# Two matrix sums change places in PSUM: the down projection of layer 0 moves from the convolution's banks to those of the transposed maxima

## Chip, cores and metric

The kernel runs on one core of one Trainium2 chip. The metric is the device time of one execution in microseconds (us). The engines are called PE (TensorE, with its weight loads as PEld), DVE (VectorE), ACT (ScalarE), POOL (GpSimd) and SP (SyncE, which issues transfers). PSUM is the memory into which PE writes and from which DVE and ACT read.

## What is computed

Two layers are applied to x, 32 graphs of 512 nodes with 256 features, with a 0/1 adjacency of 512 x 512 for each graph. The change lies in layer 0, which is a graph convolution and then a feed-forward block, each behind a layer norm and added to x. Cut to what matters:

```python
# graph convolution
h = x @ W_msg
msg_sum = einsum('bij,biu->bju', a, h);  deg = sum(a, axis=1)
out = relu(x @ W_upd + msg_sum / max(deg, 1) + bias)          # 0 for deg == 0
# feed-forward block, for each node
t = max(xx[:, None, :] + Wt[None, :, :], axis=-1) + bt         # 1024 maxima over 256 sums
trop = s * max_k(t * sl_cvx + of_cvx) + (1 - s) * min_k(t * sl_ccv + of_ccv)
classical = gelu(x @ Wc + bc);  g = sigmoid(x @ Wg + bg)
fused = g * trop + (1 - g) * classical
out = fused @ Wd + bd                                          # the down projection
```

Layer 1 (attention over typed edges, then a mixer with a scan over slices) isn't touched.

## The kernel before

Layer 0 is `layer0_sorted`. Nodes are in tiles of P = 128 rows; a group has NT = 4 tiles, 512 nodes; the 1024 features of the block are FC = 8 chunks of 128. The 32 graphs are in 4 segments of 8. A segment's nodes are first convolved, then ordered by how many of their features can hold the maximum (`put_in_order`), and then taken in 8 groups, so there are 32 groups in all. CAPS says how many rows of a table are gathered for each of a segment's tiles: 24, 9, 7, ... down to 1.

The convolution of a graph is two generators. `conv_in` loads the graph and its adjacency, norms it, and multiplies by W_msg: tiles `ph` (L403), copied to `h` by ACT (L405). `conv_out` runs over pairs of node tiles: `pu` (L421) is the product with W_upd, which DVE adds to the bias into `u` (L424); for each of the two tiles `pm` (L430) is the sum over neighbours, which DVE turns into `deg` (L433, L434) and adds to `u` (L435).

The feed-forward block of a group is three functions:

- `sums(s, g)` gathers the ordered nodes `xs` (POOL, L549), norms and transposes them (`xsp`, L573), gathers rows of the table (`best` L560, `rows` L591) and takes their maximum on DVE (`best`, L594).
- `mixed(s, g)` runs over the 8 chunks f. For each it multiplies by Wc and Wg (`clsp` and `gatep`, L619) and lets ACT apply gelu and tanh (`cls`, `gate`, L621); PE transposes the maxima of the four node tiles into `tz` (L626); ACT reads tz once for the first line of the piecewise function (`acc`, L628) and once for each bend (`past`, L632; BENDS has 6, 3, 2, 1, 1, 1, 0, 0 of them); DVE adds the bends (L633) and mixes the parts (L635 to L637) into `acc[f]`, which has one buffer for each f.
- `down(s, g)` multiplies acc by Wd, two node tiles at a time, into a tile `po` (L648: 2 tiles x 8 chunks), which DVE adds to xs (L650); SP then writes the group to `x2s` (L651).

In the text tz6 is the tile tz of chunk f = 6, acc7 the tile acc of chunk 7, and so on.

The order in which the code writes the work of a group: the loop over groups takes the first step of `mixed` of the group (clsp and gatep of f = 0), then `down` of the group before it, and then weaves the other steps of `mixed` with `sums` of the next group. The generator `woven` does that by counting steps, and a second `woven` lays the convolution of the next segment beside the whole; once all convolutions are done, the same stream goes on with the preparation of layer 1 (`following`). That is the written order. The order in which each engine gets its instructions is fixed when the program is built, and differs from it in places.

PSUM has one pool for all of layer 0, `ps`, with two buffers for each tag, and each tile of the pool has 2 KiB per partition, one bank. The tags are

- `tp`: transposes of normed nodes (lnp, xsp) and of weights,
- `mm`: the convolution's ph, pu, pm, the three tiles of `put_in_order`, a few tiles of layer 1's preparation, and po,
- `mf`: clsp and gatep,
- `tz`: the transposed maxima tz.

A tile takes a bank when the earlier tile of its tag in that bank has been read for the last time; for po this is the add at L650, for tz the last read by ACT (L628 or L632).

Of the kernel before, what the change touches and what calls it, by code (L numbers as in the profile page):

```python
# [8 lines left out]
F32 = mybir.dt.float32  # L9
# [9 lines left out]
P = 128  # L19
N = 512  # L20
D = 256
# [75 lines left out]
def layer0_sorted(tc, ident, eps, x, adj, w, x2s, ranks, over, following):  # L97
# [29 lines left out]
    with ExitStack() as ctx:  # L127
        cst = ctx.enter_context(tc.tile_pool(name="c0", bufs=1))
        dr = ctx.enter_context(tc.tile_pool(name="d0", bufs=2, space=DRAM))
        ps = ctx.enter_context(tc.tile_pool(name="p0", bufs=2, space=PSUM))  # L130
# [408 lines left out]
        def feed_forwards():  # L539
# [101 lines left out]
            def down(s, g):  # L641
                xg, acc = got.pop((s, g))
                for t0 in range(0, NT, 2):
                    po = ps.tile([P, 2, D], F32, tag="mm", name=f"po{s}_{g}_{t0}")
                    for i in range(2):
                        t = t0 + i
                        for f in range(FC):
                            nc.tensor.matmul(po[:, i, :], acc[f][:, t * P : (t + 1) * P], wd[:, f, :],  # L648
                                             start=f == 0, stop=f == FC - 1)
                    nc.vector.tensor_add(xg[:, t0 : t0 + 2, :D], xg[:, t0 : t0 + 2, :D], po)  # L650
                nc.sync.dma_start(x2s[s].rearrange("(t k p) d -> k p t d", k=NG, p=P)[g], xg[:, :, :D])  # L651
# [6 lines left out]
            for i, now in enumerate(groups):  # L658
                steps_ = mixed(*now)
                next(steps_)  # L660
                if i:
                    down(*groups[i - 1])
                yield
                more = sums(*groups[i + 1]) if i + 1 < len(groups) else iter(())
                steps = sum(1 + CAPS[n] // 4 for n in range(groups[(i + 1) % len(groups)][1], ST, NG))
                yield from woven(steps_, 9, more, steps)
            down(*groups[-1])

        def all_convs():
# [1565 lines left out]
```

## Time and profile before

| | us |
|---|---|
| median of 3 runs | 4599.11 |
| lowest and highest | 4596.14, 4614.08 |
| the profiled execution | 4612.24 |
| its span, first to last instruction | 4610.5 |

Busy times in the span: PE 4079.0 us (88%), PEld 2518.9 (55%), DVE 3368.3 (73%), ACT 2292.1 (50%), POOL 1733.9 (38%). The mean granted clock of PE is 0.950.

The stages of the span: up to 404 us the first convolutions and the tables; from 404.2 us, where the first po starts, to about 1902 us groups woven with convolutions; up to about 2114 us groups beside layer 1's preparation; up to 2498 us the last groups; after that layer 1. One group takes some 60 to 78 us while convolutions run beside it, and 53 us near the end.

The instructions of the down projection are 2048 records of matmuls of 128x128 by 128x256 on PE (a matmul in this number format leaves two records) with a median of 379 ns, overlapping, so that the 64 records of a group take 14.0 us, and 64 adds on DVE with a median of 681 ns.

How to read the lines below. A line of waits says which instruction waited for which, the total in us, how many times, and the longest. A line of the timeline has start and duration in us, the engine, the source line, the operation, the tiles written and read, how many instructions were merged into the line, and in brackets how long the engine had been idle before it and what ended that. Ends of matmuls are modelled, and a busy PE isn't PE at its peak. Half of the 64 matmul records of a group belong to the first po, half to the second.

### The profile page before, as it was taken

Reading aid. Unit: us, or ns where it says so; the run is one execution under the profiler, and the core shown is the slowest. Engines: PE = TensorE matmul, PEld = TensorE weight load, DVE = VectorE, ACT = ScalarE, POOL = GpSimd, SP = SyncE. Lnnn points to the kernel's source line nnn. Section 1 sums busy time; section 2 is a strip of 40 time slices with the busy share of each in tenths; the row PEclk is TensorE's granted clock in tenths of the full one; section 3 lists DMA queues with packets and bytes.
Section 4 is the critical chain, followed back from the end, with each engine's and each line's share of the span. In section 5 each row is a group of like instructions: output and inputs, shape, how many; then the busy total and the mean of one; then the engine's idle time right before and its main releaser. Section 6 shows DMA issues by size and latency. Waiting matters only on the chain. (4 is left out here: it accounts for less than half of the span.)

```text
span 4610.5 us, 56109 instructions
## 1 busy us (share of the span) xinstructions
PE 4079.0 (88%) x19287; PEld 2518.9 (55%) x19287; DVE 3368.3 (73%) x6944; ACT 2292.1 (50%) x4756; POOL 1733.9 (38%) x2036
## 2 busy tenths in 40 slices
PE   5668898989989899888897899999999999999987
PEld 4545665656656566555554355555555555555555
DVE  6668778877788777777775777777777776777773
ACT  2344565555655556555564444545554454454433
POOL 2356544654537444353332223223323333332220
PEclk9888999999999999998998999999999999999998
DMA  5556533654427543374431111111111111111100
GB/s 130 160 162 208 170 125 115 204 181 138 137 95 223 171 131 127 91 261 147 137 110 49 53 46 56 51 48 42 45 56 49 56 56 53 48 54 56 40 14 15
DMA packets 235099, 474.08 MB, mean 103 GB/s; under 512 B 38299, under 2 KB 114075, under 8 KB 234804
## 3 DMA queue, kind: packets, MB, share of 16 engines
q0 software_dynamic: 80256, 282.38, 19.2%
q1 hardware_dynamic: 154548, 188.02, 13.3%
q8 instruction: 154, 2.52, 0.2%
q14 instruction: 141, 1.16, 0.1%
HBM read 413.16 MB, written 57.16 MB: 102 GB/s over the span
## 5 line engine op out<-in xcount | busy, mean ns | idle before, releaser
L619 PE MATMUL clsp<-xnT,wc 128*128 128x512 f32 x1024 | 526.6, 633 | 76.5 <-ACT cls L621 56.4
L619 PE MATMUL gatep<-xnT,wg 128*128 128x512 f32 x1024 | 500.7, 608 | 3.7 <-ACT gate L621 3.4
L648 PE MATMUL po<-wd,acc 128*128 128x256 f32 x2048 | 454.2, 381 | 3.9 <-DVE acc L637 2.2
L648 PEld LDWEIGHTS po<-wd,acc 128*128 128x128 f32 x2048 | 389.8, 191 | 69.4 <-issue 12.9
L430 PE MATMUL pm<-h,adj 128*128 128x257 f32 x1024 | 294.6, 434 | 126.4 <-DVE u L435 46.7
L633 DVE SCALAR_TENSOR_TENSOR acc<-past,fld,acc 128x512 f32<-128x512 f32 x448 | 347.9, 779 | 62.7 <-ACT past L632 52.6
L1209 DVE SCALAR_TENSOR_TENSOR att<-own,other,mask 128x512 f32<-128x512 f32 x512 | 376.5, 757 | 14.1 <-DMA own<-ownd 13.8
L594 DVE SCALAR_TENSOR_TENSOR best<-rows,xs,best 128x1024 f32<-128x1024 f32 x212 | 274.2, 1296 | 148.4 <-ACT best L588 93.2
L628 ACT ACTIVATE acc<-tz,fld 128x512 f32<-128x512 f32 x256 | 198.5, 776 | 283.1 <-PE tz L626 283.1
L619 PEld LDWEIGHTS gatep<-xnT,wg 128*128 128x128 f32 x1024 | 198.8, 197 | 249.7 <-issue 209.0
L591 POOL DMA_INDIRECT rows<-table,xs x212 | 253.0, 1193 | 215.7 <-DVE best L594 160.3
L632 ACT ACTIVATE past<-tz,fld 128x512 f32<-128x512 f32 x448 | 290.7, 691 | 76.6 <-DVE acc L633 76.0
L430 PEld LDWEIGHTS pm<-h,adj 128*128 128x128 f32 x1024 | 211.7, 217 | 186.2 <-issue 106.0
L1242 PE MATMUL avp<-att,hv 128*64 128x512 f32 x1024 | 308.7, 625 | 4.2 <-DVE att L1209 4.2
L619 PEld LDWEIGHTS clsp<-xnT,wc 128*128 128x128 f32 x1024 | 188.3, 201 | 226.4 <-issue 121.3
L1330 PE MATMUL lgp<-wsl,x4T 128*128 128x512 f32 x512 | 256.0, 637 | 29.8 <-DVE mask L1081 24.3
L621 ACT ACTIVATE cls<-clsp,fld 128x512 f32<-128x512 f32 x256 | 175.1, 684 | 208.6 <-PE clsp L619 102.3
L1342 PE MATMUL yTp<-sw,x 128*128 128x512 f32 x512 | 243.7, 617 | 36.4 <-DVE sw L1337 29.0
L1150 POOL DMA_INDIRECT x<-x2s,ranks x128 | 141.6, 1106 | 345.9 <-DVE att L1209 112.3
L621 ACT ACTIVATE gate<-gatep,fld 128x512 f32<-128x512 f32 x256 | 175.4, 685 | 140.2 <-PE gatep L619 105.4
L1295 POOL TENSOR_TENSOR mu<-mu,eps 128x16 f32<-128x16 f32 x32 | 121.1, 3784 | 324.4 <-DVE mu L1294 323.2
L549 POOL DMA_INDIRECT xs<-rows_of,order x128 | 145.7, 1138 | 229.6 <-DVE acc L633 82.0
(598 smaller groups left out, 8944.0 us busy)
## 6 DMA issues: line engine op xcount, KB each, us to landing
adji<-in_adj SPq DMA_DIRECT2D x128, 256.0 KB
ai<-in_adj SPq DMA_DIRECT2D x128, 256.0 KB
own<-ownd SPq DMA_DIRECT2D x128, 256.0 KB
rows_of<-keep SPq DMA_DIRECT2D x32, 550.0 KB
x<-in_x SPq DMA_DIRECT2D x32, 512.0 KB
x2s<-xs SPq DMA_DIRECT2D x32, 512.0 KB
out<-x SPq DMA_DIRECT2D x32, 512.0 KB
rows<-table,xs POOLq DMA_INDIRECT x212
```

Source lines behind the costliest of these rows:

```text
L430: nc.tensor.matmul(pm[:, : D + 1], a[:, i, t * P : (t + 1) * P], h[:, i, :], start=i == 0, stop=i == NT - 1)
L591: nc.gpsimd.indirect_dma_start(out=row, out_offset=None, in_=table, in_offset=bass.IndirectOffsetOnAxis(ap=idxs[:, k : k + 1].bitcast(U32) ...
L594: nc.vector.scalar_tensor_tensor(m, row, vals[:, k : k + 1], m, ALU.add, ALU.max)
L619: nc.tensor.matmul(pf, wf[:, c, f * P : (f + 1) * P], xnT[:, c, :], start=c == 0, stop=c == DC - 1)
L621: nc.scalar.activation(o, pf, fn, bias=fld[:, f, bf : bf + 1], scale=1.0 if fn == AF.Gelu else 0.5)
L632: nc.scalar.activation(r, z, AF.Relu, bias=fld[:, f, AT + b : AT + b + 1])
L633: nc.vector.scalar_tensor_tensor(y, r, fld[:, f, CH + b : CH + b + 1], y, ALU.mult, ALU.add)
L648: nc.tensor.matmul(po[:, i, :], acc[f][:, t * P : (t + 1) * P], wd[:, f, :], start=f == 0, stop=f == FC - 1)
L1209: nc.vector.scalar_tensor_tensor(e, own[h], other[:, j, h : h + 1], mask[:, j, :], ALU.max, ALU.mult)
L1242: nc.tensor.matmul(pv[q][k * HO : (k + 1) * HO, :], hv[:, j, h, :HO], weighed[b, h, j], start=j == 0, stop=j == NT - 1)
L1330: nc.tensor.matmul(pf, xnT[:, c, t * P : (t + 1) * P], wsl[:, c, :], start=c == 0, stop=c == DC - 1)
L1342: nc.tensor.matmul(py, xn[:, t, c * P : (c + 1) * P], sw[:, t, :], start=t == 0, stop=t == NT - 1)
```

## The change

The tile po is taken from the tag tz instead of mm. Shape, type, matmuls, the add and everything around stay as they are:

```diff
             def down(s, g):
                 xg, acc = got.pop((s, g))
                 for t0 in range(0, NT, 2):
-                    po = ps.tile([P, 2, D], F32, tag="mm", name=f"po{s}_{g}_{t0}")
+                    po = ps.tile([P, 2, D], F32, tag="tz", name=f"po{s}_{g}_{t0}")
                     for i in range(2):
                         t = t0 + i
                         for f in range(FC):
```

Both tags have two buffers of one bank each, so the pool stays at eight banks.

## The prediction

> **What bounds the kernel now.** Layer 0 ends at about 2498 us of the span of 4610.5 us (the last add of the down projection starts at 2497.4 us), and the change touches nothing later. So I read layer 0 alone: first the busy times by stretch, then PE's waits in one stretch, then the timeline around one down projection. The chain of waits is of no use here, because it follows the end of the kernel, deep in layer 1.
>
> From the windows (length, then busy time of PE, PEld, DVE, ACT, POOL), the stretch in which convolutions and feed-forward groups are woven:
>
> ```profile
> core 0: us, PE busy (x) PEld busy (x) DVE busy (x) ACT busy (x) POOL busy (x), PEclk, DMA share, GB/s
> 404.20:1902.50 1498.30, 1355.22 (x5104) 892.80 (x5103) 1170.54 (x2327) 828.25 (x1431) 750.62 (x1006) 0.96 0.47 150
> ```
>
> PE is busy for 90% of it and idle for 143 us; DVE 78%, ACT 55%. What PE's idle time waits for, in the same stretch:
>
> ```profile
> engine line waited for: us in total, times, longest us
> PE pm L430 <- DVE xs L650: 40.4, 14, 6.0
> PE pm L430 <- DVE u L435: 35.8, 11, 6.4
> PE clsp L619 <- ACT cls L621: 23.0, 22, 2.3
> PE tz L626 <- ACT acc L628: 9.1, 11, 2.3
> PE ph L403 <- DVE xs L650: 8.7, 2, 4.4
> ```
>
> The first and fifth lines are the change's target: the convolution's matmuls pm and ph wait for the adds at L650, which empty po. The only thing that they share with po is the pair of banks of tag mm. It is 49.1 us in 16 waits, a third of PE's idle time. One of the 16 closely, first PE, then DVE, then ACT:
>
> ```profile
> 1264.37 12.68 PE L648 MATMUL po<-wd,acc 128*128 128x256 f32 x58
> 1276.88 1.89 PE L421 MATMUL pu<-w_upd,x1T 128*128 128x256 f32 x8
> 1280.45 1.98 PE L430 MATMUL pm<-h,adj 128*128 128x257 f32 x8 [1.68 <-DVE xs L650]
> 1282.27 0.60 PE L626 MATMUL tz<-ident,best 128*128 128x128 f32 x4
> ```
>
> ```profile
> 1272.80 0.68 DVE L650 TENSOR_TENSOR xs<-xs,po 128x512 f32<-128x512 f32 x1
> 1274.61 1.28 DVE L594 SCALAR_TENSOR_TENSOR best<-rows,xs,best 128x1024 f32<-128x1024 f32 x1 [1.12 <-DMA rows<-table,xs]
> 1277.20 2.51 DVE L594 SCALAR_TENSOR_TENSOR best<-rows,xs,best 128x1024 f32<-128x1024 f32 x2 [1.30 <-DMA rows<-table,xs]
> 1279.62 0.68 DVE L650 TENSOR_TENSOR xs<-xs,po 128x512 f32<-128x512 f32 x1
> 1282.47 0.16 DVE L433 TENSOR_SCALAR deg<-pm 128x1 f32<-128x1 f32 x1 [1.56 <-PE pm L430]
> ```
>
> ```profile
> 1282.91 0.78 ACT L628 ACTIVATE acc<-tz,fld 128x512 f32<-128x512 f32 x1 [10.98 <-PE tz L626]
> ```
>
> The second po is full at 1277.05 us, but its add stands in DVE's queue behind maxima (L594) that wait for gathered rows; it runs 2.6 us late. pu takes the first po's bank, pm the second's, so pm waits; then DVE waits 1.56 us for pm, and the transposes tz and ACT behind them are late too.
>
> **What the Trainium skill says.** "PSUM — Partial Sum Buffer", "Specifications (TRN2)", gives 8 banks of 2 KiB per partition. The pool has four tags of two such tiles, so all eight are taken and po can only move, not get banks of its own. The same page, "Engine vs sequencer instructions": matmuls start and complete in program order, and VectorE's queue is strictly first in, first out. The trace agrees: nothing on PE passes the waiting pm at 1280.45, and the add at 1279.62 passes no L594. "Perfetto Trace Analysis", "Optimization Strategy", says that the same gap, repeating on the engine that should be saturated, can mean too little PSUM for the next tile; the 16 waits are such a gap.
>
> **The change part by part.** No instruction is added or removed: 64 po tiles (32 groups, two each), 2048 matmul records, 64 adds of 0.68 us stay.
>
> Removed: the 16 waits. In order of time they are 3.23, 2.72, 2.63, 1.32, 4.44, 5.22, 3.48, 2.74, 2.39, 1.68, 4.30, 5.99, 2.41, 2.73, 1.15 and 2.71 us, 49.1 together. How much survives depends on what PE waits for next:
> - In four groups (3.23, 2.63, 2.39, 1.15: 9.4 us) no larger wait for DVE follows before the next group, and DVE itself waits 1.6 to 3.2 us there for pm or for past from ACT. I keep all 9.4.
> - In four groups (4.44, 5.22, 4.30, 5.99: 20.0 us), those with the many rounds of maxima, DVE is nearly as full as PE: 67.6 against 67.7 us busy in 836 to 911 us, 61.3 against 65.2 in 911 to 984. I keep half, 10.0.
> - In the other eight (19.8 us) PE waits again within about 20 us, 2.9 to 6.4 us for u at L435, and there DVE had been held by "over" at L602, which waits for the gathered xs (32.6 us in 10 waits). PE's gain mostly makes that wait longer. I keep a third, 6.6.
> Sum 26.0 us.
>
> Added: po now takes the two banks that tz6 and tz7 of its own group had. po's f=7 matmul needs acc7, which DVE makes after ACT has read tz7, and tz6 was read before, so this wait costs nothing. Behind po, tz0 of the next group takes the first po's bank and waits for the first add; tz1 waits for the second. The first add ends before the second po is full in every group (closest: it ends at 1149.21 us, and the transposes start at 1149.24), so that wait costs nothing. The second add ends up to 8.2 us after po, and tz1 is reached 3.9 us after po where only tz0, cls and gate lie between, later where convolution work does. Comparing the add's end with the start of tz1 as it stands, less the removed wait, three groups pay: 425.98 against 423.94 us (2.0), 2142.65 against 2140.36 (2.3) and 2197.74 against 2194.09 (3.7). The last, PE and DVE:
>
> ```profile
> 2194.09 0.60 PE L626 MATMUL tz<-ident,best 128*128 128x128 f32 x4
> ...
> 2200.97 3.71 PE L619 MATMUL clsp<-xnT,wc 128*128 128x512 f32 x4 [6.17 <-ACT cls L621]
> ```
>
> ```profile
> 2197.06 0.68 DVE L650 TENSOR_TENSOR xs<-xs,po 128x512 f32<-128x512 f32 x1
> ```
>
> Here, and in the second (4.24 us for cls after it), the next PE wait is longer than the new one and swallows it; if that cover were gone it is 5.9 us more. I charge 2.0.
>
> Moved: the order of work on an engine is not the written one, and it can be drawn anew. Now, transposes of the next group often run ahead of po (three of tz0, three of tz1):
>
> ```profile
> 544.96 0.49 PE L626 MATMUL tz<-ident,best 128*128 128x128 f32 x3
> 545.97 0.55 PE L626 MATMUL tz<-ident,best 128*128 128x128 f32 x3 [0.53 <-ACT acc L628]
> ```
>
> They come before the po that starts at 554.57 us. Counting the transposes before each po, 74 run ahead like this. I assume that the banks of one tag go out in the order of the code, po first; the other way both tz tiles would hold the banks, ACT could not empty them, since acc0 has one buffer that po has yet to read, and the program could not run. So the 74 fall behind po: 74 x 0.11 us (what one adds in a run of them) = 8 us of PE work, which now fills the time before po. Against it, the waits tz on acc (9.1 us, mostly this run-ahead) go, and pu, pm and ph may now be put before a po that waits. The trace can't show that order. I take zero; bounds are 9 gained and 8 lost.
>
> Net 26.0 - 2.0 = 24 us. The profiled execution takes 4612.24 us around its span of 4610.5, so it would become about 4588; it lies 13 us over the median shown, so the median goes from 4599.1 to 4575.
>
> **The rivals.**
> - Everything stays gained: PE is the bound at 90%, and 49 + 9 - 2 = 56 at most, 49 as its middle: 4550. For it: the PE share. Against it: the L435 waits and the full DVE.
> - All is absorbed: DVE and the row gathers set the pace, the stall at pm turns into waits of PE for u or cls: 4597, 10 either way. For it: 20 of the 49 us stand ahead of such waits.
> - Slower: transposes that no longer run ahead. If the new order puts tz1 right behind tz0, cls and gate, it waits for the second add wherever that starts more than 3.3 us after po's end (3.9 less 0.68): summed over the groups' present lags, 23 us. With the 8 us of transposes that is 31, and ACT and DVE, which can start acc0 only after them, pass it on; with 8 of the 49 us kept it is 23 slower, 4622. It decides once the adds lag behind po by more than these 3.3 us in most groups; today they do in 16 of 32.
>
> **How the numbers follow.** Forecast (4575, own range 4558 to 4590) 0.42; all gained 0.16; absorbed 0.22; slower 0.20. What a measurement here can tell from no change is about 0.5%, 23 us, so faster means below 4576. Of the forecast's 0.42, 0.27 lies below it; with the 0.16, faster is 0.43. Same: 0.15 of the forecast, 0.20 of absorbed, 0.03 of slower, 0.38. Slower: 0.17 and 0.02, 0.19. The range leaves out the better half of "all gained" and the worse half of "slower": 4540 to 4625.
>
> **What would show it.** Right: no wait of pm or ph on L650; waits of PE for L650 only at tz, below 10 us; the last add of L650 some 24 us before 2497; layer 1 as long as before. Waits of pm for u at L435 above 36 us show the absorbed part. Wrong: tz waiting for L650 in most groups, or PE busy before po with nothing and after it with eight transposes; or a change in layer 1's length, which would mean that the order there was redrawn.

## The result: no measurable change

The changed kernel takes 4608.6 us (median of 20 runs) beside 4609.2 us for the kernel before (20 runs). The ratio is 1.0003, with a 95% interval of 0.9994 to 1.0012. The forecast of 4575 us was 34 us too low: 10 of them because it started from a median of 3 runs, 4599.1 us, and 24 because the gain didn't come. The profiled execution has a span of 4604.4 us (4610.5 before) at nearly the same mean granted clock, 0.952 for 0.950. Layer 0 ends 9 us earlier in it (the last matmul of po ends at 2488.3 us, before at 2497.3), layer 1 takes 3 us longer.

What was meant to go is gone. First the windows over the same stretch of groups and convolutions (length, busy time of each engine), then PE's waits there, both of the changed kernel:

```profile
404.20:1902.50 1498.30, 1344.95 (x5100) 880.68 (x5099) 1175.37 (x2324) 831.05 (x1434) 757.11 (x1006) 0.96 0.47 150
```

```profile
PE pm L430 <- DVE u L435: 59.1, 16, 7.9
PE clsp L619 <- ACT cls L621: 45.6, 31, 4.8
...
PE tz L626 <- DVE xs L650: 3.1, 5, 1.6
```

The 49.1 us of pm and ph behind the adds have left, and only 3.1 us of tz behind them came. Yet PE is no busier than before (1345 us for 1355). Two other waits grew by nearly as much as was saved: pm for u at L435 from 35.8 to 59.1 us, and clsp for cls from 23.0 to 45.6 us.

The group that the prediction followed (group 12, counted from 0) shows the first of them. PE, DVE and POOL of the changed kernel, as timelines:

```profile
1276.81 1.88 PE L619 MATMUL gatep<-xnT,wg 128*128 128x512 f32 x4
1284.78 3.77 PE L430 MATMUL pm<-h,adj 128*128 128x257 f32 x8 [6.09 <-DVE u L435]
```

```profile
1266.36 0.68 DVE L650 TENSOR_TENSOR xs<-xs,po 128x512 f32<-128x512 f32 x1
...
1277.64 0.17 DVE L602 TENSOR_TENSOR over<-xs,limits 128x4 f32<-128x4 f32 x1 [5.20 <-DMA xs<-rows_of,order]
...
1284.16 0.48 DVE L435 SCALAR_TENSOR_TENSOR u<-pm,deg,u 128x256 f32<-128x256 f32 x1
```

```profile
1270.75 0.95 POOL L549 DMA_INDIRECT xs<-rows_of,order  x1 [10.48 <-DVE acc L633]
```

The same compare and the same pm in the kernel before:

```profile
1291.65 0.17 DVE L602 TENSOR_TENSOR over<-xs,limits 128x4 f32<-128x4 f32 x1 [4.03 <-DMA xs<-rows_of,order]
```

```profile
1298.78 3.77 PE L430 MATMUL pm<-h,adj 128*128 128x257 f32 x8 [4.92 <-DVE u L435]
```

Read the changed kernel's lines upwards. The matmul pm waits 6.09 us for u, which is a 0.48 us operation. It stands in DVE's queue behind the compare `over` at L602, 0.17 us long, and behind 6.4 us of other work that piled up after it, while the compare itself stood 5.20 us waiting for the rows xs of a later group. POOL could issue the gather of those rows at 1270.75 us only. The bracket names an acc of DVE, but xs has three buffers, so the rows of group 15 need the one of group 12, whose adds must be done and whose write (L651) must have left: in both kernels the gather starts 3.69 us after SP issues that write (1267.06 and 1270.75 after, 1280.34 and 1284.03 before). So the stall at the adds and this one are links of one chain that starts with the second add: from that add to the compare it takes 12.0 us before (1279.62 to 1291.65) and 11.3 us after (1266.36 to 1277.64). When the add comes earlier, the compare comes as much earlier, but PE, which has lost its first pause, arrives earlier too, and waits here: 6.09 us, where it had waited 4.92.

### The profile page after: what moved, and what is told of

It reads as the page before. It is cut to its first block, busy times and chain, and to the rows that moved or that the text cites. A ratio compares the mean times of both kernels' runs of the same rounds, so it can differ in the third digit from the quotient of the medians.

```text
span 4604.4 us, 56098 instructions
## 1 busy us (share of the span) xinstructions
PE 4069.8 (88%) x19287; PEld 2509.9 (55%) x19287; DVE 3368.6 (73%) x6944; ACT 2291.6 (50%) x4756; POOL 1741.5 (38%) x2036
## 5 line engine op out<-in xcount | busy, mean ns | idle before, releaser
L619 PE MATMUL clsp<-xnT,wc 128*128 128x512 f32 x1024 | 524.9, 633 | 85.4 <-ACT cls L621 70.2
```

Source lines behind the costliest of these rows:

```text
L619: nc.tensor.matmul(pf, wf[:, c, f * P : (f + 1) * P], xnT[:, c, :], start=c == 0, stop=c == DC - 1)
```

## The experiments

The recorded expectations name theories by letters, each with what it claims. The main ones are A (the compare at L602 takes the place of the stall), D (DVE is too full to let anything be gained), G (the stall is worth some 30 us, and sharing the bank tz costs as much; its opposite F says that L602 absorbs all of it), with two ideas of where that cost lies: G2 and G2a (transposes and classifier products no longer run ahead of po) and G3 (the order on the engines is drawn anew in layer 1's preparation). Each ratio is against the kernel before on the same chip, with its 95% interval. Where two kernels are compared by their ratios, the two intervals leave about 10 us either way (an estimate from them).

### The compare, PE and a third way to empty po

Two kernels without the compare at L602: its flags are set to zero once, so the marking of nodes that need more rows than were gathered is left out. One starts from the kernel before (b_noover), the other from the changed one (a_noover).

```diff
-                nc.vector.tensor_tensor(over[...], xg[:, :, COUNT], limits[...], ALU.is_gt)
...
             got = {}
+            nc.gpsimd.memset(over[:, : B * NT], 0.0)
```

> The kernel before without the compare at L602 (leaves out the flags of rows whose list was too short; they are set to zero instead). It takes away the place where DVE waits for the gathered xs (67.4 us in 18 waits), nothing else. Theory A (PE's gain from the change is absorbed because DVE stands at L602, in a chain of fixed length that starts at the second add of po): PE's waits of pm for u at L435 fall from 46.7 to under 25 us and the time falls by 15 to 40 us. Theory B (PE is the bound, and the change gave back its gain by its own costs: transposes that no longer run ahead, waits at tz): the time stays within 8 us. Theory C (DVE and the row gathers are the bound as a whole, L602 is one wait among many): L602's time goes to other DVE waits, less than 10 us gained.

> The changed kernel without the compare at L602 (leaves out the same flags). Theory A: with the place of absorption gone, the change is worth something: a_noover is faster than b_noover by 10 to 25 us (the 19.8 us of the eight groups, and part of the rest). Theory B: it equals b_noover within 5 us, as the change's own costs are still there, and both equal the kernel before. Theory C: a_noover equals b_noover within 5 us, both up to 10 us faster than before.

Measured: 4531.2 us for b_noover, ratio 0.9845 (0.983 to 0.986), 72 us less than before; 4521.2 us for a_noover, 0.9826 (0.9811 to 0.9841). The wait behind the compare is worth more than the stall, and more than expected. In the kernel before, DVE spends 67.4 us of the whole span in it, 18 times, and taking it away gave back all of that and a little more. Without it pm waits for u only this long in the stretch of the windows (b_noover):

```profile
PE pm L430 <- DVE u L435: 4.1, 6, 1.8
```

The 72 us are also twice those 35.8 us that PE waits for u in the stretch (46.7 in the whole span). A wait of PE can cost more than its length here. The pm behind the wait of 6.09 us shown above took 3.77 us for its 8 records, at a granted clock of 0.50; the pm at 1265.36 us, behind no wait, took 1.90. In the kernel before, 18 of the 19 pm of layer 0 from 404 us on that had waited 2.4 us or more, with their 8 records in one piece, took 3.0 to 3.8 us, and the 4 that had waited 1.2 to 2.2 us took 1.98. In b_noover 3 of the 9 that had waited as long took 1.98 all the same, so the length alone doesn't decide it. From the end of po in group 0 to that in group 20, b_noover takes 60 us less than before (1364.5 for 1424.4), and 29 of them are PE's busy time, 1262.6 us at a mean clock of 0.98 for 1291.8 at 0.96, with 4875 records in both. The prediction priced each wait at its length. This is read from single profiles; no run varies the clock by itself.

But the compare isn't why the change gained nothing. With the compare gone from both, the change brings 10 us, with intervals that overlap, not the 24 forecast or the 49 that PE waits. So A is a large part of the kernel's time and only a part of the answer.

To see whether PE sets the pace by itself, b_pu2 issues the matmuls pu twice, some 110 us more of PE's work.

```diff
-                for k in range(2):
+                for k in (0, 1, 0, 1):
```

> The kernel before with the four matmuls of each pu (L421) issued twice, so 1.7 us more of PE work for each of 64 pu tiles, about 54 of them beside feed-forward groups, some 95 us there and 110 us in all, none of it on another engine. It prices PE's time in this stage from the other side. Theory A: part of it lies before waits that shrink by as much: 30 to 70 us slower. Theory B (PE is the bound): 85 to 115 us slower. Theory C (DVE and gathers are the bound): under 30 us slower.

Measured: 4669.2 us, 1.0145 (1.0127 to 1.0162), so 66 us more for 110. PE's busy time rose by 85 us only (4164.4 for 4079.0, at a mean clock of 0.956 for 0.950), so some of the 110 was made up by faster matmuls and some fell into pauses. DVE's wait behind the compare didn't shrink; in the same windows it went from 32.6 us in 10 waits to this (b_pu2):

```profile
DVE over L602 <- DMA xs<-rows_of,order: 69.1, 14, 7.0
```

In b_act po stays in mm, ACT copies it out and POOL does the adds.

```diff
-                    nc.vector.tensor_add(xg[:, t0 : t0 + 2, :D], xg[:, t0 : t0 + 2, :D], po)
+                    half = sb.tile([P, 2, D], F32, tag="past", name=..., bufs=3)
+                    nc.scalar.copy(half, po)
+                    nc.gpsimd.tensor_add(xg[:, t0 : t0 + 2, :D], xg[:, t0 : t0 + 2, :D], half)
```

> The kernel before, po still in mm, but emptied by ACT into a buffer of tag past and added to xs by POOL, so that po's bank doesn't wait for DVE's queue: the same stall of pm is taken away without touching tz, DVE is relieved of 64 adds of 0.68 us (44 us), and the write of x2s, the load of the next xs and L602 start earlier. Theory A: the chain to L602 starts up to 3 us earlier in each group and the stall is gone, 20 to 50 us faster. Theory B: 30 to 50 us faster, for the stall is gone and no run-ahead is lost. Theory C: about as much as DVE is relieved where it is full, 15 to 30 us. If the waits of pm for po stay, on ACT or POOL instead of DVE, it says nothing.

Measured: 4617.3 us, 1.003 (1.0019 to 1.004). It tells nothing of the bank, since it changed other things too: the adds now stand in POOL's queue with the gathers of rows, the maxima on DVE wait 46.7 us for rows in the stretch, 34.7 before, and DVE waits 43.5 us at the compare, 32.6 before.

### Is DVE too full?

b_dve2 and a_dve2 are b_noover and a_noover with the three mixing operations (L635 to L637) left out for f = 6 and 7, which takes 131 us of work from DVE.

```diff
+                    if f < 6:
                     nc.vector.tensor_sub(y, y, out["cls"])
...
```

> b_noover with less work for DVE: the three mixing operations of the chunks f = 6 and 7 (of 8) are left out, so the output leaves out their gates; 6 x 0.68 us in each of 32 groups, 131 us of DVE, nothing of PE or ACT. Theory D (DVE's queue is the pace: freed PE time only moves PE's waits to others that end with DVE): 60 to 120 us faster than b_noover (4531), waits of pm for the adds of po stay at 25 us or more. Theory B (PE is the bound and the change has costs of its own): at most 40 us faster than b_noover.

> The same cut of DVE's work (gates of f = 6 and 7 left out) in a_noover, so the change under a relieved DVE. Theory D: PE becomes the pace, and the change is worth more than under the full DVE: a_dve2 is 20 to 50 us faster than b_dve2, where a_noover was only 10 faster than b_noover. Theory B: the change's own costs are still there, so a_dve2 is within 12 us of b_dve2.

Measured: 4506.6 us, 0.9795 (0.9782 to 0.9809), and 4504.7 us, 0.9787 (0.9774 to 0.9801). Against their parents that is 23 and 18 us (by the ratios) for 131 us of work, far from D's expectation of 60 to 120; and with a lighter DVE the change is worth 2 us, inside the intervals, where D wanted 20 to 50. D falls.

### The same stall, removed without the bank tz

bn_copy2 is b_noover, but ACT copies po into a tile of the tag past and DVE adds from there. po stays in mm, its bank comes free without DVE's queue, and tz isn't touched. b_copy makes the same edit in the kernel before, with the compare in place and nothing left out; an_copy is bn_copy2 with po in tz.

```diff
-                    nc.vector.tensor_add(xg[:, t0 : t0 + 2, :D], xg[:, t0 : t0 + 2, :D], po)
+                    half = sb.tile([P, 2, D], F32, tag="past", name=..., bufs=3)
+                    nc.scalar.copy(half, po)
+                    nc.vector.tensor_add(xg[:, t0 : t0 + 2, :D], xg[:, t0 : t0 + 2, :D], half)
```

> b_noover with po left in mm, but copied by ACT into a buffer of tag past, from which DVE adds it to xs. ACT frees the bank, so the stall of pm and ph (48.6 us in b_noover) goes without tz being touched and with the transposes still running ahead; DVE's adds stay. It takes the change's benefit without its costs. Theory D: within 15 us of b_noover, as for a_noover. Theory B: 30 to 50 us faster than b_noover, 20 or more faster than a_noover (4521).

> The kernel before, L602 in place, with ACT copying po out of mm (as in bn_copy2). It prices the removal of the stall itself in the kernel that the change was made to. Theory F (L602 absorbs the stall's removal there, tz's sharing costs little): 4590 to 4605, no gain over before. Theory G (the stall's removal is worth its 25 to 35 us there too, and the change lost them by sharing tz): 4565 to 4578.

> a_noover (po in tz, no L602) with ACT copying po out of its bank, so that tz no longer waits for DVE's late adds, while the transposes still can't run ahead of po. Theory G1 (the own cost of the change is the wait of tz for the adds): near bn_copy2 (4502), under 4508. Theory G2 (the own cost is that transposes no longer run ahead, or that the order of work was redrawn with it): near a_noover, 4514 to 4525.

| kernel | compare | po in | emptied by | us | ratio (95%) |
|---|---|---|---|---|---|
| after | yes | tz | DVE | 4608.6 | 1.0003 (0.9994 to 1.0012) |
| b_copy | yes | mm | ACT | 4570.3 | 0.9928 (0.9907 to 0.9948) |
| b_noover | no | mm | DVE | 4531.2 | 0.9845 (0.983 to 0.986) |
| a_noover | no | tz | DVE | 4521.2 | 0.9826 (0.9811 to 0.9841) |
| an_copy | no | tz | ACT | 4522.5 | 0.9831 (0.981 to 0.9851) |
| bn_copy2 | no | mm | ACT | 4502.0 | 0.9776 (0.9762 to 0.979) |

Three things follow. Removing the stall this way is worth 33 us in the full kernel (b_copy) and 32 without the compare (bn_copy2 against b_noover), 64 copies of ACT included: the forecast's 26 was not too high, and F falls. The bank tz costs 25 us without the compare, where only the bank differs (an_copy against bn_copy2). In the full kernel the changed kernel lies 34 us above b_copy, but there the engine that empties po differs too; no kernel with the compare had po in tz and ACT's copy. And an_copy equals a_noover, so without the compare it doesn't matter which engine empties po in tz, and the transposes' wait for the adds, which ACT's copy makes independent of DVE's queue, is not that cost. PE's waits in the stretch, in b_copy:

```profile
PE pm L430 <- DVE u L435: 41.4, 10, 7.5
PE clsp L619 <- ACT cls L621: 39.6, 25, 8.2
```

Both grew here too, by 5.6 and 16.6 us, but in the changed kernel it was 23.3 and 22.6: with po in mm and ACT's copy, 22 of the 49 us come back as these two waits, and with po in tz 46. Not all of the 49 had left in b_copy: pm's 40.4 us did, while ph waits 6.7 us for ACT's copy where it had waited 8.7 for the adds.

### What the bank costs, and the order

In the kernel before, 76 transposes of a next group are executed before the last matmul of po (74 before its first), in the changed kernel none. bn_copy_behind leaves po in mm and only ties the transposes tz0 and tz1 behind the last matmul of po of the group before. behind_to20 and behind_from21 tie them for the po of groups 0 to 20 alone (convolutions) and of groups from 21 on alone (layer 1's preparation and later).

```diff
+                    with tc.issue_after(got["po"].ins) if f < 2 and "po" in got else ExitStack():
                         for t in range(NT):
                             nc.tensor.transpose(pt[:, t, :], best[t][:, f * P : (f + 1) * P], ident)
```

> bn_copy2 (po in mm, copied by ACT, no L602) with an order edge alone: the transposes of tz0 and tz1 of a group come on PE behind the last matmul of the po of the group before. It takes the running ahead away and leaves the banks as they were. Theory G2: 4514 to 4525, so most of the 19 us between bn_copy2 and a_noover. Theory G1: within 6 us of bn_copy2 (4502).

> As bn_copy2 (no compare on the loaded rows, the sums copied out of the convolution's bank by ScalarE), with an order edge that holds the first two transposes of a group behind the last matmul of the output product of the group before, for output products of groups 0 to 20 alone; the preparation of layer 1 (groups 21 to 24) keeps its order. Theory G2a (the own cost of sharing the bank tz is that transposes and classifier products no longer run ahead of po, and it falls among the convolutions, groups 5 to 20): most of the 24 us of the edge in all groups stays, 4514 to 4525 us. Theory G3 (it is that the written order is drawn anew, and most of it falls in groups 21 to 24): within 8 us of bn_copy2, 4500 to 4511 us.

> The other part of the same edge: only behind output products of groups 21 and later. Theory G2a: as bn_copy2, 4502 give or take 6 us. Theory G3: 12 to 20 us more than bn_copy2.

Measured: 4526.2 us, 0.983 (0.981 to 0.9849), for the tie in all groups; 4512.6 us, 0.9804 (0.9785 to 0.9824), for groups to 20; 4516.5 us, 0.9812 (0.9793 to 0.9831), for the rest. Against 0.9776 (0.9762 to 0.979) of bn_copy2 these are 25, 13 and 17 us; only the interval for groups to 20 still touches bn_copy2's. The order alone, with no bank shared, costs as much as the bank does, within the error. It seems to cost in both stages, so neither G2a nor G3 had it whole.

The order of bn_copy_behind is not that of the changed kernel in every respect: there PE also begins po earlier and mixes other work into it (36.1 us from the first to the last matmul of po in group 6, 14.0 before, 14.1 in bn_copy_behind). And much of the cost is not idle time. Between the profiles of bn_copy2 and bn_copy_behind the span grows by 30 us and PE's busy time by 21 (4031.6 to 4052.3 us, mean clock 0.959 and 0.955), between b_copy and the changed kernel by 34 and 17 (4053.1 to 4069.8), with 19287 records in each: the same matmuls took longer, as behind the waits above.

Then the bank itself, by stage: an_copy and the changed kernel with po in tz for groups 0 to 20 only, in mm after.

```diff
-                    po = ps.tile([P, 2, D], F32, tag="tz", name=...)
+                    po = ps.tile([P, 2, D], F32, tag="tz" if groups.index((s, g)) <= 20 else "mm", name=...)
```

> As an_copy (no compare, ScalarE's copy, po in bank tz), but po takes tz only in groups 0 to 20 and mm from group 21 on. Theory G2a: the 20 us that an_copy lies above bn_copy2 stay for the most part, 4515 to 4522 us. Theory G3: half or more of them go, 4502 to 4513 us.

> The whole changed kernel, with po in tz in groups 0 to 20 alone and in mm after. Theory G2a: no gain, within 6 us of the kernel before. Theory G3: 8 to 15 us faster than before.

Measured: 4518.5 us, 0.9815 (0.9799 to 0.983), 7 us better than an_copy with intervals that overlap; and 4608.4 us, 1.0008 (1.0 to 1.0017), no gain at all. The second doesn't tell where the bank's cost lies: with po in mm and emptied by DVE from group 21 on, the stall is back there together with the run-ahead. One profile each of the changed kernel and b_copy says more. From the end of po in group 0 to that in group 20 they take 1425.6 and 1400.3 us, from there to group 24, beside layer 1's preparation, 285.3 and 276.6: most of the difference lies among the convolutions, and a part does not.

Last, where among them. In one profile of each kernel I took the time from the end of a group's po to the end of the next. After groups 6 and 14 it is 80.4 and 83.7 us in the changed kernel, 72.6 and 71.7 before, 70.0 and 72.5 in b_copy, 81.5 and 80.6 in an_copy. In bn_copy_behind it is 77.3 and 81.9, in bn_copy2 71.0 and 71.3, although clsp of two chunks runs ahead of these po in both: here the transposes make the difference. So po was put back into mm in these two groups alone, in an_copy (an_copy_not2) and in the changed kernel (tz_not2):

```diff
+                    po = ps.tile([P, 2, D], F32, tag="mm" if groups.index((s, g)) in (6, 14) else "tz", name=...)
```

> As an_copy (no compare, ScalarE's copy, po in bank tz), but po takes mm in groups 6 and 14 alone, the two after which every kernel that holds the transposes behind po takes 80 us where the others take 71. Theory G2a, narrow form (the loss sits in these two groups, because transposes and classifier products of the next group ran ahead of their po): the stretches after groups 6 and 14 go back to 71 to 73 us each, 15 to 20 us in all, 4503 to 4510 us. Otherwise (the loss is spread, or moves on to other groups): 4516 to 4524 us.

> The whole changed kernel with po in mm in groups 6 and 14 alone and in tz in all others. Theory G2a, narrow form: the stretches after these groups go from 80 and 84 back to about 73 us, and the kernel is 10 to 20 us faster than before. Otherwise: within 6 us of before, as the change itself.

Measured: 4512.8 us, 0.9808 (0.9789 to 0.9826), for an_copy_not2; 4594.8 us, 0.998 (0.9972 to 0.9987), for tz_not2. Each is some 10 us better than its parent, for 2 of 32 groups; for tz_not2 the intervals lie apart, for an_copy_not2 they overlap. The stretches after these groups fell to 70.2 and 71.3 us in tz_not2, those before them grew by 4 each. Both missed the narrow form of G2a: an_copy_not2, for which it wanted 15 to 20 us, and narrowly tz_not2, 9 us faster than before where it wanted 10 to 20.

PE's waits from the end of po in group 5 to the end of po in group 7 show what the order did there. First the changed kernel (152.9 us long), then tz_not2 (146.6 us):

```profile
PE clsp L619 <- ACT cls L621: 4.1, 2, 3.3
...
PE lnpa L60 <- ACT xnT L601: 2.3, 1, 2.3
```

```profile
PE ph L403 <- DVE xs L650: 3.2, 1, 3.2
...
```

And from the end of po in group 13 to that in group 15, the changed kernel (158.8 us) and tz_not2 (150.6 us):

```profile
PE clsp L619 <- ACT cls L621: 11.0, 6, 4.5
PE lnpa L60 <- ACT xnT L601: 3.8, 1, 3.8
```

```profile
PE clsp L619 <- ACT cls L621: 5.6, 4, 2.2
PE ph L403 <- DVE xs L650: 4.3, 1, 4.3
```

With po in mm the stall at the adds is back (3.2 and 4.3 us at ph), and still the pair is shorter, because the waits for ACT's cls go from 15.1 to 5.6 us together (none is left in the first pair) and those for xnT from 6.1 to nothing; PE's busy time falls by another 5 us. The timelines of ACT show how. First the changed kernel, then tz_not2:

```profile
841.14 1.58 ACT L452 ACTIVATE xnb<-keep,shiftb,rsb 128x256 f32<-128x256 f32 x3 [23.39 <-DVE shiftb L446]
...
848.63 0.68 ACT L621 ACTIVATE cls<-clsp,fld 128x512 f32<-128x512 f32 x1
```

```profile
825.12 0.69 ACT L621 ACTIVATE cls<-clsp,fld 128x512 f32<-128x512 f32 x1 [1.99 <-PE clsp L619]
...
841.72 0.60 ACT L452 ACTIVATE xnb<-keep,shiftb,rsb 128x256 f32<-128x256 f32 x1 [15.42 <-DVE shiftb L446]
```

In tz_not2 PE had fed ACT a chunk of the next group ahead of po, and its cls is done at 826 us. In the changed kernel ACT stands for 23 us behind an instruction of the sorting (L452) that waits for DVE, and PE, which works off po until 837 us, gives it no transposes before 840.46; then ACT has everything to do at once, and PE's next clsp waits 3.3 us for the cls at 848.63 to free its bank. That is read from the trace of these groups. The runs show only that the bank in these two groups costs 10 us, net of the stall that came back there.

### What beats both

a_late2 is the changed kernel with the compare moved behind the second add of `down`, where its rows have long landed. The kernel "both" is the kernel before with ACT's copy and the moved compare. Both leave nothing out.

```diff
-                    nc.vector.tensor_add(xg[:, t0 : t0 + 2, :D], xg[:, t0 : t0 + 2, :D], po)
+                    half = sb.tile([P, 2, D], F32, tag="past", name=..., bufs=3)
+                    nc.scalar.copy(half, po)
+                    last = nc.vector.tensor_add(xg[:, t0 : t0 + 2, :D], xg[:, t0 : t0 + 2, :D], half)
+                with tc.issue_after(last.ins):
+                    nc.vector.tensor_tensor(over[...], xg[:, :, COUNT], limits[...], ALU.is_gt)
```

> The changed kernel with the whole computation: the compare of L602 is kept, but written in down behind the second add of the group's po, with an order edge, so that it comes when its xs has long landed. If L602 cost its 72 us only by standing in DVE's queue before its rows had landed, this gives nearly all of what leaving it out gave: 4515 to 4535, against 4521 for a_noover. If the compare itself or the traffic was the cost, it stays above 4580.

> A version with the whole computation: po stays in mm, ACT copies it out, and the compare of L602 comes behind the second add (as in a_late2). It should come near bn_copy2, 4498 to 4512, faster than before by some 2%; if the late compare costs as much as the early one in this order, above 4530.

Measured: 4526.0 us, 0.9838 (0.9824 to 0.9851), and 4511.4 us, 0.9804 (0.9781 to 0.9827). The second is 90 us faster than the kernel before, and both times lie in the expected ranges.

## Why the prediction was wrong, step by step

- **Removed** (49.1 us of waits, 26 kept): right in mechanism, and the size held. b_copy removes nearly the same waits and gains 33 us, with an interval from 24 to 43.
- **A third kept in the eight groups ahead of `over` at L602**: the group shown above agrees in kind: 6.09 us of wait for u where there had been 4.92. The step saw that wait as a shelter for what is gained. It didn't see that the wait behind the compare is itself worth 72 us, twice what PE waits for it in the stretch.
- **Half kept in the groups where DVE is full**: not tried by itself. With 131 us less on DVE the kernels gained 18 and 23 us, so the fullness weighs less than I took it to.
- **Added** (tz1 behind the second add, 2.0 us): about right. The profile shows 3.1 us in 5 waits in the stretch, and an_copy, where DVE's queue no longer stands between po and its bank, is no faster than a_noover.
- **Moved** (the transposes that ran ahead; "I take zero; bounds are 9 gained and 8 lost"): this is the step that failed. That they fall behind po was right, 76 before and none after. Their price was taken as that of their own PE time, 74 times 0.11 us, and then set to zero. Measured, it is 25 us without the compare (an_copy against bn_copy2), and 25 for the order alone (bn_copy_behind); in the full kernel the changed kernel lies 34 us above b_copy, bank and emptying engine together. What ran ahead was not 8 us of filler: the tz of the next group are the head of ACT's and DVE's work on it. In the groups followed above, lateness there made a later clsp wait for ACT; how the other groups pass it on was not followed. The rival "slower" named this ("ACT and DVE, which can start acc0 only after them, pass it on") and put it at 31 us, but tied it to a wait of tz1 for the adds, which didn't come, and to only 8 us kept of the stall.
- **The sum**: some 33 gained and 34 lost. The rival "absorbed" foretold no change, and its sign came (59.1 us of pm for u, above 36), but for another reason: DVE and the gathers took back only a part, since b_copy gained 33 us with the compare in place.

What is open: of the 34 us, 10 are shown to sit in groups 6 and 14, net of the stall there. Without the compare some 7 may sit in layer 1's preparation, within the error. No run divides the other part further, and the order alone was not tried with the compare in place. How much of each cost comes by waits and how much by slower matmuls is read from single profiles only. b_copy also adds 64 copies to ACT and takes turns in the buffers of past, so its 33 us are what this removal is worth, not the stall free of all else.

The Trainium skill, "Perfetto Trace Analysis", "Optimization Strategy", says to find what blocks the gaps of the engine that is to be saturated and to let those dependencies start sooner. Here the largest such gap in the stretch, 49.1 us in pm and ph, was worth 33. The next, 35.8 us of pm for u, led to a wait in another engine's queue that was worth 72.

## What to carry to other kernels

A tile that moves to another tag of a PSUM pool takes a place in that tag's order: ask which instructions ran ahead through these buffers and whom they feed, and price the lateness of what they feed, not their own time alone. If a bank only needs to come free sooner, let an engine with time to spare copy it out before giving it neighbours. A tiny operation that waits for a prefetched transfer belongs where its data has long landed, not where the code first has the tile.

## Not expected of the hardware

A compare of 0.17 us in VectorE's in-order queue, 32 of them, held the kernel up by 72 us of 4603, by waiting for a gather (67.4 us in 18 waits). That agrees with the Trainium skill, "PSUM — Partial Sum Buffer", "Engine vs sequencer instructions", by which VectorE's queue is strictly first in, first out; its price I hadn't expected. About half of what the compare's removal gained among the convolutions is not waiting but the same matmuls in less time, at a mean clock of 0.98 for 0.96. And with PE busy 90% of the stretch, 110 us more work on it cost 66, while 131 us less on DVE, busy 78%, gained 18 to 23 in the kernels without the compare: neither engine's share told what its work is worth.
